# A gated two-block kernel: the first weight group of the first feed-forward is rounded four plan steps and fetched five plan steps further on in the prologue

## The chip, the core and the metric

The kernel runs on one core of a Trainium2 chip. The metric is the device time of one execution in microseconds (us); several executions are timed and the median is taken. Engines are named as the profile names them: PE (matrix products), PEld (its weight loads), DVE (vector), ACT (scalar functions), POOL, and SP, whose queue issues nearly all transfers. A name with a q behind it (SPq, DVEq) is that engine's instruction queue.

## What is computed

Four batches of 512 tokens with 512 features pass through two blocks. Each block adds a gated attention-like term and then a gated feed-forward term to the residual x:

```python
x = x + tanh(g_xattn[0]) * xattn0(layernorm(x), ctx, W_k, b_k, ln_gamma, ln_beta)
x = x + tanh(g_ffn[0])   * ffn0(layernorm(x), up, up_bias, down, down_bias)   # weights rounded to 4 bits
x = x + tanh(g_xattn[1]) * xattn1(layernorm(x), ctx, Wq, Wkv, Wout)           # 16 causal heads
x = x + tanh(g_ffn[1])   * ffn1(layernorm(x), W1, W2, W3)                     # silu gate, Hadamard
```

The part that matters here is `ffn0`. Its up matrix (512 x 2048) and its down matrix (2048 x 512) are rounded first: in each block of 32 along the contraction axis the largest absolute value gives a power-of-two scale, and every weight is rounded to a signed 4-bit grid times that scale.

## The kernel before

The weights of `ffn0` are taken in four groups of 512 hidden units. For each group, `quantise(n)` (L485) is a generator whose steps are interleaved with other work. Its first step fetches the raw rows from memory by 16 transfers of 128 KB (L508) into two tiles, half 0 and half 1. Two steps then find the block maxima on DVE (L525 to L534), one for each half. Eight more steps round four quarters k = 0 to 3, two steps for each quarter: the first does L549 to L552, the second L556 to L559. After the quarters 1 and 3 the rounded half is stored to a scratch matrix `qw_d` in memory by eight transfers (L566). `fetch_q(n)` (L571) then loads the two rounded matrices back in the layout that PE wants, as `up_q` and `dn_q`, 1 MB each (L576). The feed-forward's first product in each chunk, `pu`, reads `up_q` and its second, `acc`, reads `dn_q`. The store, the load back and the raw rows of the next group are all on SP's queue, in one order, and the two raw tiles exist once: the rows of group 1 can be fetched into a half only when the stores of that half of group 0 have landed.

The stretch before the first feed-forward product is the prologue. It runs four generators `cross0(b)` (L663), one for each batch, which do the whole first cross-attention of a batch; `keys_values` (L838), which computes the keys and values of the second attention for later and stores them by SP (`k_d`, `v_d`) out of the tiles `kk_ghi`, `kk_glo` (two of each), `spare` and `vv` (two); and `q0 = quantise(0)`. Two steps of the crosses 0, 1 and 2 and one of keys and of q0 (its fetch) are taken ahead. The rest is written out as a plan (L941 to L951): for each k from 0 to 22, one step of cross 0, of cross 1 from k = 3, of cross 2 from k = 6, of cross 3 from k = 10, then of q0, then one or two steps of keys. `in_time(plan, 20)` (L918) traces the plan's entries in that order and ties each entry, on each of PE, DVE, ACT and POOL, behind the last instruction that was traced on that engine up to the entry 20 places before. SP is not tied. Within these ties a scheduler with a simulated timeline orders each engine; earlier traced work goes first among what is ready.

Cross b has, in the order of its steps: context transposes; tokens 0; key projection; tokens 1; key transposes; tokens 2; the Gram matrix with tokens 3 and the variance (L750); `po` (L753); `pg_o` with the product on DVE (L760); the row scales, a chain of small DVE operations that ends at L778; their transpose; four score tiles `v` with their maximum on DVE (L792) and exponential on ACT (L796); the residual update (L809); squares (L818); scaling; and the layernorm's rows and four transposes. Cross 0's last step is at k = 22.

After the plan, `ffn0((0,), 0, (1, 5))` (L956) starts on batch 0 and group 0. Its first product `pu` goes into a PSUM bank that cross 2 used before (the two banks "h"). Beside its chunks run the steps of `quantise(1)`, one for each chunk, and the rest of the crosses and keys. The tiles of `up_q` take turns with `spare` and the transposed key weights, and the tiles `ghi`, `glo` of the feed-forward are those of `kk_ghi`, `kk_glo`.

Of the kernel before, what the change touches and what calls it, by code (L numbers as in the profile page):

```python
# [42 lines left out]
def flamingo_kernel(  # L43
# [410 lines left out]
    with ExitStack() as l0:  # L454
# [180 lines left out]
        with ExitStack() as xa:  # L635
# [300 lines left out]
            def fetched(n):  # L936
                fetch_q(n)
                yield
# [3 lines left out]
            for k in range(23):  # L942
                plan.extend([crosses[b] for b in range(NB) if k >= 3 * b + b // 3])
                if k == 6:
                    plan.extend([crosses[3]] * 2)
                if k > 4:
                    plan.append(q0)
                if k == 14:
                    plan.append(fetched(0))

                plan.extend([keys] * (2 if 1 < k < 11 else 1))  # L951
# [205 lines left out]
    with ExitStack() as l1:  # L1157
# [191 lines left out]
        with ExitStack() as at:  # L1349
# [238 lines left out]
            with tc.manual_schedule(engines={nc.tensor.engine}):  # L1588
                for s in range(-4, 4 * last + 2):
                    n, g = divmod(s, 4)  # L1590

                    u, k = divmod(s + 8, 4)
# [324 lines left out]
```

## Time and profile before

| | before |
|---|---|
| median of 3 runs | 1300.35 us (1293.84 to 1302.87) |
| profiled execution: its time | 1300.33 us |
| its span, from first to last instruction | 1298.6 us |
| PE busy | 1209.8 us, 93% of the span |
| DVE busy | 846.9 us, 65% |
| ACT busy | 551.6 us, 42% |
| DMA, mean | 144 GB/s |
| q0's first maximum on DVE (L525) | from 24.41 us |
| q0's last rounding operation (L559) | 72.08 to 73.30 us |
| load back of up_q / dn_q issued | 81.91 / 84.42 us |
| first feed-forward product (`pu`) | 118.13 us |

The profile is one execution on the chip. Times are counted from the span's start. Busy time of PE is modelled, so a busy PE is not a PE at its peak. In a row of the timeline the columns are start, duration, engine, line, operation, output<-inputs, shapes and count; a bracket at its end gives the idle time of the engine just before it and what ended it. The chain is the work that ended last, followed back from the end, with start, duration and what it was.

### The profile page before, as it was taken

The numbers are of one execution on the slowest core, as the hardware profiler recorded it, in microseconds if no ns is written. First come the engines' busy times: TensorE is split into PE (matmuls) and PEld (weight loads), VectorE is DVE, ScalarE is ACT, GpSimd is POOL, SyncE is SP. The second block draws the span as 40 slices with busy tenths as digits, with TensorE's granted clock in tenths as the row PEclk, the third lists the DMA queues.
The fourth block names the chain that finished last, engine by engine and source line by source line (L and its number), as shares of the span: only waits on it lengthen the run. The fifth ranks groups of instructions, "written<-read, shape, count | busy, mean of one in ns | idle before, by whom it ended". The sixth has DMA issues, their size and how long they took to land.

```text
span 1298.6 us, 17523 instructions
## 1 busy us (share of the span) xinstructions
PE 1209.8 (93%) x6097; PEld 906.8 (70%) x6097; DVE 846.9 (65%) x1772; ACT 551.6 (42%) x1040; POOL 350.6 (27%) x480
## 2 busy tenths in 40 slices
PE   5998899999999899898989799999999999999998
PEld 4545677878677675565646477777777788888886
DVE  5876897896947665455455656777677754555556
ACT  4559742333433455454445742444334632122210
POOL 1000010000000235445344133444444533333330
PEclk9999999999999899898998799999999999999999
DMA  8792575354153655355340144554434544433421
GB/s 202 282 237 100 73 150 134 98 146 130 25 165 121 190 160 160 101 155 146 93 127 10 49 162 179 195 195 162 172 145 159 222 160 172 171 146 146 154 82 65
DMA packets 113203, 186.43 MB, mean 144 GB/s; under 512 B 13229, under 2 KB 65581, under 8 KB 107995
## 3 DMA queue, kind: packets, MB, share of 16 engines
q1 hardware_dynamic: 110754, 185.04, 45.4%
q8 instruction: 48, 0.79, 0.3%
q10 hardware_dynamic: 2360, 0.28, 0.2%
q14 instruction: 41, 0.33, 0.1%
HBM read 109.22 MB, written 75.80 MB: 142 GB/s over the span
## 4 chain that ended last, share of the span: by engine, by line
PE 64%; DVE 13%; DMA 10%; ACT 6%; issue 2%; SPq 2%; POOL 1%; DVEq 0%; ACTq 0%; POOLq 0%
PE acc L135 12%; PE pS L135 11%; PE pA L135 9%; PE pu L135 5%; PE pp L140 4%; PE acc L595 3%; PE sT L1404 3%; PE sc L409 3%; PE pav L1436 3%; PE den L1444 2%; PE pq L140 2%; DMA w_d<-fw 2%; DMA q_d<-qq 1%; DMA k_d<-kk_glo 1%; DVE fw L284 1%
## 5 line engine op out<-in xcount | busy, mean ns | idle before, releaser
L135 PE MATMUL pS<-tok,pack 128*128 128x512 f32 x768 | 194.8, 399 | 0.0
L135 PE MATMUL acc<-w2T,gg 128*128 128x512 f32 x768 | 183.9, 392 | 5.7 <-DVE x L1790 5.5
L135 PEld LDWEIGHTS acc<-w2T,gg 128*128 128x128 f32 x768 | 142.9, 188 | 39.1 <-DVE x L1790 9.5
L135 PEld LDWEIGHTS pS<-tok,pack 128*128 128x128 f32 x768 | 142.8, 189 | 32.9
L135 PE MATMUL pA<-tok,pack 128*128 128x512 f32 x576 | 152.8, 404 | 0.0
L1790 DVE SCALAR_TENSOR_TENSOR x<-acc,tg,x 128x512 f32<-128x512 f32 x128 | 95.7, 749 | 63.8 <-PE acc L135 63.4
L135 PE MATMUL pu<-xnT,up_q 128*128 128x512 f32 x512 | 131.0, 401 | 6.1 <-DMA up_q<-qw_d 2.3
L420 DVE CUSTOM_DVE_ANT_0 junk<-sc,mask 128x512 f32<-128x512 f32 (+1 forms) x128 | 79.5, 621 | 81.0 <-PE sc L409 76.7
L1408 ACT ACTIVATE e<-sT 128x384 f32<-128x384 f32 (+1 forms) x192 | 95.4, 524 | 76.3 <-PE sT L1404 73.3
L135 PEld LDWEIGHTS pA<-tok,pack 128*128 128x128 f32 x576 | 109.1, 192 | 24.5
L135 PEld LDWEIGHTS pu<-xnT,up_q 128*128 128x128 f32 x512 | 96.0, 190 | 30.1 <-issue 3.0
L1414 POOL TENSOR_SCALAR_AFFINE_SELECT e<-e 128x128 f32<-128x128 f32 (+1 forms) x192 | 62.6, 331 | 143.6 <-ACT e L1408 140.8
L1832 ACT CAST gg<-s 128x512 fp32r<-128x512 f32 x64 | 39.7, 622 | 109.5 <-POOL s L1829 96.9
L409 PE MATMUL sc<-stk 96*128 96x128 f32 (+3 forms) x256 | 80.7, 357 | 5.8 <-ACT e L1408 1.9
L1829 POOL TENSOR_TENSOR s<-s,p 128x512 f32<-128x512 f32 x15 | 19.7, 1316 | 241.4 <-DVE p L1827 137.4
L1404 PE MATMUL sT<-stk 98*128 98x512 f32 (+3 forms) x256 | 80.7, 360 | 3.1 <-ACT e L1408 2.6
L1833 POOL TENSOR_TENSOR gg<-s,gg 128x512 fp32r<-128x512 f32 x60 | 77.2, 1304 | 6.8 <-ACT gg L1832 6.8
L595 PE MATMUL acc<-dn_q,glo 128*128 128x512 f32 x192 | 75.8, 395 | 1.0 <-DVE glo L618 1.0
L614 ACT ACTIVATE ghi<-pu,up_b 128x512 fp32r<-128x512 f32 x48 | 33.1, 689 | 101.0 <-PE acc L595 82.4
L595 PE MATMUL acc<-dn_q,ghi 128*128 128x512 f32 x192 | 75.4, 393 | 0.0
L1404 PEld LDWEIGHTS sT<-stk 98*128 98x128 f32 x256 | 46.1, 196 | 31.7 <-issue 12.8
L1822 ACT ACTIVATE s<-s 128x512 f32<-128x512 f32 x64 | 40.4, 632 | 51.9 <-DVE s L1821 51.7
(290 smaller groups left out, 2208.9 us busy)
## 6 DMA issues: line engine op xcount, KB each, us to landing
pack_d<-pack SPq DMA_DIRECT2D x16, 1024.0 KB
pack<-pack_d SPq DMA_DIRECT2D x16, 1024.0 KB
pack_d<-pack SPq DMA_DIRECT2D x16, 768.0 KB
pack<-pack_d SPq DMA_DIRECT2D x16, 768.0 KB
qw_d<-qw SPq DMA_DIRECT2D x64, 128.0 KB
q_d<-qq SPq DMA_DIRECT2D x16, 512.0 KB
st<-in_L_ffn_W_dram SPq DMA_DIRECT2D x32, 256.0 KB
w2T_d<-w2T SPq DMA_DIRECT2D x16, 512.0 KB
```

The costliest lines, as they stand in the source:

```text
L135: nc.tensor.matmul(out, a, b, start=(i == 0), stop=(i == len(terms) - 1))
L140: nc.tensor.matmul(out, a, b, start=(i == 0), stop=(i == len(terms) - 1))
L409: nc.tensor.matmul(sc[:, g, :], qst[:96, g0 + g, ts(i, P)], kst[:96, g0 + g, :w], start=(g == 0), stop=(per == 1),)
L420: nc.vector.tensor_tensor_reduce(junk[:, :w], sc[:, 0, :], mask[:, S - w :], 1.0, -3.0e38, ALU.add, ALU.max, fin[:, i, g0 : g0 + 1],)
L595: nc.tensor.matmul(acc[t], g[:, ts(t, P)], dn[:, f % 4, :], start=(f == chunks[0] and i == 0), stop=(f == chunks[-1] and i == 1 and groups ...
L1404: nc.tensor.matmul(sc[:, at_ : at_ + S - j * P], kst[:98, g, ts(j, P)], qst[:98, g, j * P :], start=True, stop=True,)
L1408: nc.scalar.activation(e[:, ds(EOFF[js[0]], w)], sc, AF.Exp)
L1414: nc.gpsimd.affine_select(diag, diag, [[0, len(js)], [1, P]], ALU.is_ge, 0.0, base=0, channel_multiplier=-1,)
L1790: nc.vector.scalar_tensor_tensor(x[b][:, t, :], acc, tg[:, 3:4], x[b][:, t, :], ALU.mult, ALU.add)
L1822: nc.scalar.activation(s, s, AF.Silu)
L1832: nc.scalar.copy(g[:, 0], s)
L1833: eng.tensor_sub(g[:, 1], s, f32(g[:, 0]))
```

## The change

Two conditions of the plan are changed, and nothing else.

```diff
                 plan.extend([crosses[b] for b in range(NB) if k >= 3 * b + b // 3])
                 if k == 6:
                     plan.extend([crosses[3]] * 2)
-                if k > 4:
+                if k > 8:
                     plan.append(q0)
-                if k == 14:
+                if k == 19:
                     plan.append(fetched(0))
 
                 plan.extend([keys] * (2 if 1 < k < 11 else 1))
```

The ten steps of q0 stand at k = 9 to 18 and no longer at k = 5 to 14, with all that they issue: the two maxima, the eight rounding steps, and 16 stores to `qw_d`, eight after k = 14 and eight after k = 18 (before: after 10 and 14). The two loads of `fetch_q(0)` stand at k = 19 and no longer at 14. Once q0 is at its end, its entries in the plan are empty but still count among the 20 of `in_time`; the plan is four entries shorter (122 for 126). The fetch of q0's raw rows stays ahead of the plan.

## The prediction

> **What bounds the kernel now.** I read the slices of the page first, then the chain over 68 to 119 us, then the timelines of ACT, DVE, SP and PE there. Slices of 32.5 us, busy time in tenths, the first four of which are the prologue:
>
> ```profile
> PE   5998899999999899898989799999999999999998
> DVE  5876897896947665455455656777677754555556
> ACT  4559742333433455454445742444334632122210
> DMA  8792575354153655355340144554434544433421
> ```
>
> From 32 us on PE is at 8 or 9 tenths nearly everywhere, so a time won or lost before the first feed-forward product is carried to the end almost whole, and nothing else is touched: no operation is added or removed. The question is what the move does to the start of `pu` at 118.13 us. DVE is fullest in the second slice, where q0 runs now; the DMA is at 9 in the third (q0's stores, the load back, the rows of group 1) and at 2 in the fourth. The chain through the third slice:
>
> ```profile
> 72.40 6.11 DMA k_d<-kk_glo
> ...
> 80.96 3.41 DMA qw_d<-qw
> ...
> 84.84 11.00 DMA qw<-in_L_ffn_up_kernel_dram
> 95.85 2.67 DMA qw<-n_L_ffn_down_kernel_dram
> 98.53 0.60 ACT kk_ghi L121
> ```
>
> Every DMA piece here is q0's own traffic or a key store behind it. Where the engines feel it (ACT twice, then the first `pu`):
>
> ```profile
> 77.95 0.59 ACT L121 CAST kk_ghi<-pk 128x512 fp32r<-128x512 f32 x1 [1.94 <-DMA k_d<-kk_ghi]
> ...
> 98.05 0.59 ACT L874 COPY vv<-pv 128x512 f32<-128x512 f32 x1 [3.08 <-DMA v_d<-vv]
> ```
>
> ```profile
> 118.13 2.13 PE L135 MATMUL pu<-xnT,up_q 128*128 128x512 f32 x8 [1.83 <-ACT xT L796]
> ```
>
> So `pu` waits for cross 2's exponentials to give back its bank, not for the weights: these were asked for at 81.91.
>
> **The change, part by part.** *The front, 22 to 57 us: 0 (from -2 to 0).* By the tie of 20 entries, q0's first maximum now comes behind cross 0's variance L750. In the row of before that is at 21.84 and the maximum at 24.41, after a wait of 2.21 for its rows, so it can stay. The second maximum moves behind the key split `spare` of batch 1 (43.78 for 30.04). This frees some 2.4 us of DVE around 30 to 40, which buys nothing: ACT stands idle from 32.85 to 38.64 until a `k_d` store has landed, and from 40 to 57 PE has no gap. If that cover were gone, 2 us could be won: the idle 2.39 of PE before 26.36, most of it q0's maximum ahead of a `spare` split.
>
> *The middle: the wait at 77.95.* The key store is queued on SP behind the rows of group 1 (issued 68.06 to 71.8). These need the stores of half 0, which now follow the sixth q0 step at k = 14, so they come later; but the eight stores of half 0 take their place at about 72 to 77 beside the same key stores. DVE stood idle 3.42 us there. I take half, -1.7 (from -3.4 to 0), as the transfers that come are 1 MB like those that leave.
>
> *The wait at 98.05.* The `v_d` store was issued at 89.94, behind up_q, dn_q and five transfers of rows; some 3 MB. In their new places only the rows of half 0 (1 MB, 8 issues of about 0.45 us, now on the move until about 77, as the DMA's rate is 135 to 139 GB/s from 70 to 76 and 308 after) come before 95 us, about 80 to 92. I take the wait as gone: -3.1 (from -5.4, all of PE's gaps between 94 and 100, to 0).
>
> *DVE at 80 to 105.* Three rounding steps come here that were done by 73: one first half (0.69 + 0.69 + 0.43 + 0.43 = 2.24) and two second halves (0.43 + 0.69 + 0.69 + 1.22 = 3.03), 8.3 us. By the five slices of 5 us DVE is idle 2.32 + 1.22 + 0 + 2.95 + 0.13 = 6.6 us there. The 1.7 over go onto the small chains of the crosses, which feed ACT, and ACT is full from 98 on: +2 (0, if the idle time serves, to +4.6, if the 2.95 before 100 goes with the stall).
>
> *When the weights arrive.* The tenth q0 step now comes behind cross 2's L778, the end of its row scales:
>
> ```profile
> 72.08 1.22 DVE L559 TENSOR_TENSOR qw<-qc,qcols 128x1024 f32<-128x1024 bf16 x1
> ...
> 102.23 0.16 DVE L778 TENSOR_TENSOR rows<-var,hi 128x4 f32<-128x4 f32 x1
> ```
>
> The first is q0's last operation now. From 102.23 go the 1.7 above and the 2.76 that DVE idles inside that chain before 99.15; the ninth step adds 2.24 into it, the tenth itself 3.03: q0 ends at 103.0 for 73.3. From there to the landing of up_q the trace has the same sequence for group 1: L559 ends at 185.67, then
>
> ```profile
> 185.70 4.35 SPq L566 DMA_DIRECT2D qw_d<-qw  x8
> 190.21 0.40 SPq L576 DMA_DIRECT2D up_q<-qw_d  x1
> 192.51 0.38 SPq L576 DMA_DIRECT2D dn_q<-qw_d  x1
> ```
>
> ```profile
> 197.42 3.07 PE L135 MATMUL pu<-xnT,up_q 128*128 128x512 f32 x9 [2.32 <-DMA up_q<-qw_d]
> ```
>
> 11.7 us. So up_q lands at 114.7; `acc` needs dn_q 6.5 us after the first `pu` (124.63 for 118.13), and dn_q is issued 2.3 us after up_q. If `pu` is to start at 116.3, that leaves 1.6 us: 0 here, but of 30 us of slack almost nothing is left. If L778 gains nothing and both steps and the small chain share DVE (102.23 + 2.24 + 3.03 + 4.5), q0 ends at 112 and up_q lands at 123.7: +5.6. The bounds are 0 and +5.6; the ties are hard and the stall is seen, so I stay at the lower.
>
> *Behind it on SP.* In front of up_q wait the eight stores; behind it now come key stores of batch 3 (issued 102.92 to 104.8), value stores, and the rows of group 1, half 1. Two `ghi`/`glo` tiles of the first chunks (ACT 120.64) are the last `kk` tiles: +1 (0 to +5.8, the longest such wait, at 38.64). The rows of half 1 took 13.7 us from issue at 84.84 to 98.53; issued at 118 they land at 131.7, and L525 wants them at 133.13: 0 (to +3). POOL issues no transfers; ACT's queue issues none after 5.6 us.
>
> **Sum:** -1.7 - 3.1 + 2 + 0 + 1 = -1.8 on 1300.33, the profiled execution's own time, which is the median of the runs (1300.35): 1298.5 us.
>
> [...] The rows: PE is busy 1.55 of the 5 us from 95, and the granted clock of the next 5 us is 0.68. [...]
>
> **The rivals.** *The weights come late (slower).* The place is the first `pu`, the price one us for each us that q0 ends after 118.13 - 11.7 = 106.4. For it: the tie behind cross 2's L778, DVE without spare time at 90 to 95 and 100 to 105, and SP in one order. Against it: DVE idles 1.4 to 2.7 us in each slice after 105, so the tenth step isn't held up for long. With q0 at its end at 115 up_q lands at 126.7, +8.6: 1309. Over 1% (13 us) it takes an end after 119.4.
>
> *The DVE and DMA relief comes whole (faster).* Both waits go (-3.4 and -3.1), the front gives its -2 and the crowding is hidden in what remains: -8.5, 1291.8. For it: the DMA has 2 tenths in the fourth slice to take the traffic. Against it: 16 stores and 18 loads still pass between the same key and value stores, only later.
>
> *Little moves.* The plan is an order of tracing; within the ties the scheduler may put q0 back into DVE's idle time, with its first five steps near their old times. Then the third slice stays as it is: 1300.3. Against it: the ties of the steps 8 to 10 are at 79 to 102 us.
>
> **How the numbers follow.** Forecast 0.55; late weights 0.27; whole relief 0.10; little moves 0.08. A measurement of this kernel can tell about 1%, 13 us, from no change. The forecast and the third rival are within it. Of the late weights I put 0.11 beyond +13 us; of the relief 0.04 beyond -13, where the clock of the rule and PE's other gaps before 40 us would have to come too. Faster 0.04, same 0.85, slower 0.11. The range reaches from the whole relief to the late end at 115, each with the 2.5 us by which the highest run of before lies over the median: 1289 to 1312; outside lie some 0.05 below and 0.12 above.
>
> **What would show it.** Right: q0's last L559 ends at 100 to 106, up_q is issued at 107 to 111, no wait of ACT for `v_d` near 98, `pu` at 114 to 119 and still released by ACT. Wrong: `pu` released by the DMA of up_q and more than 3 us after 118; a `ghi` or DVE's L525 of group 1 waiting for a DMA at 118 to 135; or q0 ending before 85. The forecast fails as a whole if the span moves by more than `pu` does, for then the scheduler has set a later stage otherwise.

## The result, and the profile after

The change made the kernel slightly slower. The changed kernel took 1306.63 us in the median of 20 runs (1299.48 to 1310.74), the kernel before 1300.23 us (1293.84 to 1306.90, 20 runs): ratio 1.0039, 95% interval 1.0023 to 1.0055. Run again in another series it gave 1.0043 (1.0023 to 1.0064). The forecast was 1298.5 us, no difference. The profiled execution of the changed kernel is one of its quick ones: 1302.32 us, span 1300.6.

The slices of its page show where the first 230 us differ; PEclk is the clock granted to PE. Each column is 32.5 us:

```profile
PE   5998889999999899898989789999999999999998
...
DVE  5688879996847665555455546777676754555556
...
PEclk8998989999999899898998789999999999999999
DMA  9766195354143655455340135554444644444421
```

The DMA's peak has gone from the third slice to the fourth, DVE's work has moved likewise: the move took place. The clock row of before has no 8 in its first 13 slices; this one has three in its first six.

The prologue first. The DVE timeline shows q0's last rounding operation, SP's the traffic behind it, PE's the first product:

```profile
104.83 1.22 DVE L559 TENSOR_TENSOR qw<-qc,qcols 128x1024 f32<-128x1024 bf16 x1
```

```profile
106.07 4.37 SPq L566 DMA_DIRECT2D qw_d<-qw  x8
110.61 0.38 SPq L576 DMA_DIRECT2D up_q<-qw_d  x1
```

```profile
118.96 2.10 PE L135 MATMUL pu<-xnT,up_q 128*128 128x512 f32 x8 [1.88 <-DMA up_q<-qw_d]
```

q0 ends at 106.05 us and no longer at 73.30, the load back goes out at 110.61 and no longer at 81.91, and yet `pu` starts only 0.83 us later (118.13 before). Of the slack nothing is left: the releaser is now `up_q`. The 0.83 us are no more than executions differ by: in the six profiles of this case with the prologue of before `pu` starts at 115.4 to 119.4 us, in six with the changed one at 116.8 to 119.6.

Behind `pu` PE is then even ahead: batch 1's residual update ends at 166.33 us, for 169.17 before. The loss comes after that. The timeline of PE for batch 3's layernorm transposes and first products, before:

```profile
174.11 1.03 PE L259 MATMUL pt_f<-ident,xn_f 128*128 128x128 f32 x8
176.82 1.35 PE L259 MATMUL pt_f<-ident,xn_f 128*128 128x128 f32 x8
182.10 5.74 PE L135 MATMUL pu<-xnT,up_q 128*128 128x512 f32 x24
```

and after:

```profile
180.15 1.09 PE L259 MATMUL pt_f<-ident,xn_f 128*128 128x128 f32 x8
184.17 1.94 PE L259 MATMUL pt_f<-ident,xn_f 128*128 128x128 f32 x8 [2.93 <-DVE xnT L122]
187.51 8.42 PE L135 MATMUL pu<-xnT,up_q 128*128 128x512 f32 x24 [1.40 <-DVE xnT L122]
```

Before, the transposes stood among batch 2's `acc` products and nobody waited for them. After, they stand behind the last of these, with nothing else for PE to do: 2.93 and 1.40 us of idle time, and the 24 products behind them take 8.42 us for 5.74. The windows of the two kernels there (columns: PE, PEld, DVE, ACT, POOL busy in 5 us, granted clock, DMA share, GB/s) say why, before:

```profile
180.00:185.00 5.00, 5.00 (x22) 3.60 (x21) 4.97 (x8) 0.74 (x2) 3.69 (x10) 1.00 0.24 43
185.00:190.00 5.00, 5.00 (x24) 4.15 (x23) 4.72 (x9) 2.10 (x4) 0.00 (x0) 1.00 0.57 131
```

after:

```profile
180.00:185.00 5.00, 2.07 (x13) 1.72 (x13) 4.62 (x7) 2.48 (x4) 0.00 (x0) 0.80 1.23 144
185.00:190.00 5.00, 3.60 (x12) 2.71 (x11) 1.38 (x2) 1.17 (x2) 3.82 (x14) 0.50 1.15 203
190.00:195.00 5.00, 5.00 (x17) 3.92 (x16) 2.34 (x3) 2.13 (x4) 0.55 (x2) 0.67 0.93 266
```

PE's share of work falls to 2.07 of 5 us and the clock that is granted next is 0.50, then 0.67. Why the layernorm is late is seen on DVE, in the chain of cross 3's residual update. Before:

```profile
148.15 0.18 DVE L801 RECIPROCAL ssum<-ssum 128x4 f32<-128x4 f32 x1 [1.33 <-ACT xT L796]
...
149.02 0.75 DVE L809 SCALAR_TENSOR_TENSOR x<-xT,ssum,x 128x512 f32<-128x512 f32 x1
```

after:

```profile
149.43 0.18 DVE L801 RECIPROCAL ssum<-ssum 128x4 f32<-128x4 f32 x1 [0.61 <-ACT xT L796]
151.43 0.69 DVE L618 TENSOR_TENSOR glo<-g,ghi 128x512 fp32r<-128x512 f32 x1 [1.82 <-ACT g L616]
...
153.37 0.74 DVE L809 SCALAR_TENSOR_TENSOR x<-xT,ssum,x 128x512 f32<-128x512 f32 x1
```

The scheduler, which had another state of its timeline at the end of the prologue, put a `glo` of the feed-forward between the reciprocal and the update. DVE waits there 1.82 us for ACT, whose `ACT_TABLE_LOAD` takes 1.28 us from 149.41 on, between the two uses of one `pu`, and the update is 4.35 us later. By the end of the layernorm's chain of small operations (L223 at 177.19 for 170.49) it is 6.7 us.

A second place stands far behind, where the second attention passes into the second feed-forward. The order of PE, DVE and ACT differs there in some twenty places, and one wait of PE shows it, before:

```profile
748.34 5.04 PE L140 MATMUL pp<-woT,oT 128*128 128x512 f32 x14 [0.79 <-DVE tok L122]
```

after:

```profile
751.35 7.20 PE L140 MATMUL pp<-woT,oT 128*128 128x512 f32 x20 [2.39 <-DVE tok L122]
```

### The profile page after: what moved, and what is told of

It reads as the page before. It is cut to its first block, busy times and chain, and to the rows that moved or that the text cites. A ratio compares the mean times of both kernels' runs of the same rounds, so it can differ in the third digit from the quotient of the medians.

```text
span 1300.6 us, 17524 instructions
## 1 busy us (share of the span) xinstructions
PE 1214.7 (93%) x6097; PEld 909.5 (70%) x6097; DVE 847.3 (65%) x1772; ACT 552.1 (42%) x1040; POOL 349.3 (27%) x480
```

## The experiments

Four theories run through them. P: the prologue itself costs the time. In the first expectations it is called W (the weights come late). L: batch 3's late layernorm. S: the passage at 737 to 770 us, called the passage below. F came up on the way: the gap at the front of the prologue and the one at 181 to 187, each with a half clock behind it (in the changed kernel 0.50 from 26.01 to 32.84 us and from 183.02 to 193.26; some expectations call it cold). O, named in one expectation, says only that the later orders decide and not the prologue. All were timed against the kernel before on the same chip.

**One step in place of four.**

```diff
-                if k > 4:
+                if k > 5:
...
-                if k == 14:
+                if k == 15:
```

> q0's rounding begins one plan step further on than before (k > 5) and its load back is one step further on (k == 15): a quarter of the change. In the program's order on PE this kernel nevertheless has the four transposes of batch 3's layernorm behind the last `acc` product of batch 2, as the changed kernel has, where before they stand between batch 2's products. Theory L (the loss comes from batch 3's layernorm, late on DVE and so behind batch 2 on PE): the whole loss of the change, +5 us on 1300 (ratio 1.004, from 1.002 to 1.006), and the first `pu` of batch 3 starts 4 to 6 us later than before's 182.10. Theory W (the loss comes from the weights: each step by which the rounding and the load back are late costs its share): a quarter, +1 us (ratio 1.001). Theory S (the loss comes from the other order of the products where the second attention passes into the second feed-forward): this kernel has before's order there, so 0.

Measured: 1310.15 us, ratio 1.0058 (1.0035 to 1.0081). A quarter of the change costs no less than the whole, so the loss isn't counted by the steps. Batch 3's first `pu` is late, with the same two waits ahead of it as in the changed kernel (2.93 and 1.40):

```profile
193.79 8.39 PE L135 MATMUL pu<-xnT,up_q 128*128 128x512 f32 x24 [1.40 <-DVE xnT L122]
```

It was 11.7 us later than before, where 4 to 6 were expected; of these some 4 had been lost by batch 1's end (173.14 for 169.17).

**One step, load back two steps on; two steps, load back three.** The first:

```diff
-                if k > 4:
+                if k > 5:
...
-                if k == 14:
+                if k == 16:
```

> As the one-step kernel (k > 5), but with the load back two steps further on (k == 16) in place of one. Its order on PE has batch 3's layernorm transposes between batch 2's products, as before, and at the passage from the second attention to the second feed-forward the order of the changed kernel. Theory L: no loss, ratio 1.000 (0.998 to 1.002), the first `pu` of batch 3 within 2 us of before's 182.10. Theory W: +1 to +2 us, more than the one-step kernel, since the load back is later. Theory S: the whole loss, +5 us (1.004).

Measured: 1305.64 us, 1.0030 (1.0007 to 1.0052). Batch 3's first `pu` starts at 183.43, as theory L said, but there is a loss. Its passage has the changed kernel's order, and a wait of 2.39 us stands before `pp`. That speaks for a second cause, S.

The second:

```diff
-                if k > 4:
+                if k > 6:
...
-                if k == 14:
+                if k == 17:
```

> The rounding begins two steps further on (k > 6), the load back three (k == 17): about half of the change. The order on PE has batch 3's layernorm transposes between batch 2's products, as before, and at the passage to the second feed-forward it is that of before. Theory L: no loss, ratio 1.000 (0.998 to 1.002; a gain of up to 2 us is possible, since the DMA waits in the prologue shrink), the first `pu` of batch 3 within 2 us of 182.10. Theory W: half of the loss, +2.5 us (1.002), more than the one-step kernel. Theory S: 0.

Measured: 1306.98 us, 1.0042 (1.0023 to 1.0061). This was a miss for theory L: neither of the two orders is that of the changed kernel, and it is as slow. The profile shows another loss, in the prologue: its first `pu` starts at 130.07 us, 11.9 later than before. That profile is of the slowest of its twelve runs (1313.96 us), so how much of this the others lost there is open. Each of these settings is a schedule of its own.

**The load back alone.** q0's rounding stays where it was.

```diff
-                if k == 14:
+                if k == 19:
```

> One half of the change alone: the load back is moved to k = 19 and q0's rounding stays at its old place (k > 4). On PE batch 3's layernorm transposes stand between batch 2's products, as before, and on DVE q0's first maximum is as near the front as before. Theory F (new: two gaps of PE make the loss, each with the cold clock behind it: one at 23 to 27 us, where q0's first maximum stands on DVE ahead of a key split and waits for the raw rows, 4.21 us in the changed kernel against 2.39 before, the other at 181 to 187 us, batch 3's layernorm): 0, ratio 1.000 (0.998 to 1.002). Theory W (lateness of the weights): +1 to +3 us, if the first `pu` then waits for up_q. A ratio over 1.003 would speak against both.

Measured: 1310.95 us, 1.0072 (1.0047 to 1.0098), against all theories. The first `pu`:

```profile
129.63 2.91 PE L135 MATMUL pu<-xnT,up_q 128*128 128x512 f32 x8 [2.52 <-DVE xnT L122]
```

It is 11.5 us late, but not for the weights: its `up_q` went out at 82.70, 0.79 us later than before, and the releaser is DVE's last operation of a layernorm. PE is busy for 1.12 of the 5 us from 100 on and runs at a clock of 0.50 in the next five. So moving two transfers in the plan moved the crosses too.

**Equal turns beside the feed-forward, prologue of the change kept.**

```diff
-            jobs.append(both(crosses[1], both(*crosses[2:], keys)))
+            jobs.append(both(*crosses[1:], keys))
```

> The changed kernel with its prologue untouched; only the turns of the work beside the first feed-forward are dealt out otherwise: crosses 1, 2, 3 and keys one step each in turn, where before cross 1 had every second turn and crosses 2, 3 and keys a sixth each. Cross 3's residual update and layernorm are traced earlier, and its transposes stand between batch 2's products on PE again. Theory L: the loss goes: ratio 1.000 against before (0.997 to 1.002), that is 4 to 7 us under the changed kernel, and the first `pu` of batch 3 at 180 to 184 us. Theory W: the prologue is as late as in the changed kernel, so +5 us (1.004) stays. Theory S: this kernel has before's order at the passage, so 0; the place of batch 3's first `pu` tells it from theory L.

Measured: 1302.55 us, 1.0008 (0.9985 to 1.0030). In this kernel q0 ends at 106.08 and up_q is asked for at 110.72, as late as in the changed kernel; the layernorm is early again, and from 290 us on PE, DVE and ACT have the order of before:

```profile
181.77 5.74 PE L135 MATMUL pu<-xnT,up_q 128*128 128x512 f32 x24
```

The loss is gone. Repeated later:

> The changed kernel with equal turns once more, beside these three: the changed prologue, and neither of the two orders behind it. Theories L and S: 1.001 (0.999 to 1.003). Theory P: 1.004.

Measured: 1300.19 us, 0.9998 (0.9977 to 1.0018). Whether the equal turns hide a loss by a gain of their own was asked by giving them to the kernel before:

> Control for the equal turns: the kernel before, with nothing but the turns of the work beside the first feed-forward dealt out equally to crosses 1, 2, 3 and keys. Theory L and theory F: in before batch 3's layernorm is not late, so the equal turns bring nothing: ratio 1.000 (0.998 to 1.002). If instead the equal turns are a gain by themselves, 0.996 to 0.998, then the kernel with the change and equal turns (1.0008) still holds a loss of 3 to 5 us, and the place of batch 3's layernorm was not the cause.

Measured: 1305.08 us, 1.0026 (1.0008 to 1.0045): no gain but a loss. Its profile is 3 us ahead of before at 540 us and 4 us behind after 760. From 200 us on PE's order is that of before; DVE's differs near 430 and ACT's near 610 and 690. One transposition more at the start of the second attention gives ACT its old order:

> The kernel before with equal turns, which in its profile was 3 to 4 us ahead of before from 200 to 580 us and 4 us behind at the end, with one extra 128 x 128 transposition at the start of the second attention, behind which ACT's order in the attention is that of before (three pairs of instructions no longer swapped). Theory O (the later orders, not the prologue, decide these few us): the lead survives, ratio 0.997 to 0.999. If the lead is lost to the clock's phase and not to the order: 1.002 to 1.003 as without the transposition.

Measured: 1302.28 us, 1.0008 (0.9977 to 1.0038). The lead doesn't come back in the time, and its own profile has no lead at 540 us (1.7 us behind), though up to there the two kernels have one order but for the transposition: the lead was that of one execution. The two intervals overlap, so whether those swaps cost anything stays open.

**The front.** In the profile of the changed kernel PE stands idle for 4.21 us before the third key product, in that of before for 2.39. In both q0's first maximum, which waits for the raw rows, is ahead of a key split on DVE. That maximum was tied further back:

```diff
+            def held(job):
+                with behind(traced()):
+                    next(job)
+                yield
...
-                    plan.append(q0)
+                    plan.append(held(q0) if k == 9 else q0)
```

> The changed kernel, with the first entry of q0 in the plan (k = 9, the first block maximum) tied behind the last instruction traced on each engine until then, and no longer only behind the entry 20 places before. On DVE it moves from before the first `spare` split to behind the second. Theory F: the gap of PE before the third key product (4.21 us, 23.28 to 27.49 in the changed kernel) goes or falls under 1.5 us, the granted clock from 25 to 35 us comes back from 0.60 and 0.72 to over 0.9, and the time falls by 2 to 5 us: ratio against before 1.001 (0.999 to 1.003). Theory L: that gap is caught up by the first `pu`, the loss stays at 1.004, with batch 3's first `pu` at 186 to 189 us. Theory W: 1.004.

Measured: 1306.00 us, 1.0035 (1.0010 to 1.0060). The gap is gone from where it was and stands, longer, a few products further on:

```profile
31.68 1.12 PE L716 MATMUL pc<-ident,c_sb 128*128 128x128 f32 x4 [6.14 <-DMA c_sb<-in_ctx_dram]
```

The front waits for transfers in both places (PE here, DVE's first maximum for 4.73 us in the changed kernel), and the place of the maximum is not what makes the gap. What a gap there costs at the end this run can't tell, since there still is one. Nor is a longer gap shown to come with the change: before the third key product it is 2.39 to 4.96 us in six profiles with the prologue of before, 2.78 to 5.52 in six with the changed one. With both remedies (the two diffs together):

> Both remedies in the changed kernel: the first block maximum tied as in the run with the held maximum, and equal turns beside the first feed-forward. Theory F: both gaps are gone and what the change wins in the prologue's middle is left: ratio 0.997 to 0.999 against before, 1297 to 1300 us. Theory L: as equal turns alone, 1.001 (0.999 to 1.003). Theory W: 1.004.

Measured: 1302.88 us, 1.0004 (0.9983 to 1.0024): as with the equal turns alone.

**The passage by itself.** One extra 128 x 128 transposition at the 60th of the steps of the second attention shifts the scheduler's timeline just enough to change its choice at the passage, and nothing before it. The same line gives the kernel before the changed kernel's order, and the changed kernel that of before:

```diff
-                    head = head_at(s)
+                    head = head_at(s); pn = side([P, P], "pn") if s == 60 else None; [nc.tensor.transpose(pn, ident, ident) for _ in range(1 if s == 60 else 0)]
```

> The kernel before, with one extra 128 x 128 transposition into a spare bank late in the second attention (0.15 us of PE). It shifts nothing in the program's order up to there; behind it, where the second attention passes into the second feed-forward (some 737 to 770 us), PE, DVE and ACT take the order of the changed kernel. Theory S (a part of the loss lies at this passage, where the changed kernel has a wait of PE of 2.39 us before `pp` and a cold clock behind it): +1 to +4 us, ratio 1.001 to 1.003. Theories L and F (all of the loss lies before 200 us): 1.000 (0.9985 to 1.0015).

Measured: 1304.69 us, 1.0029 (1.0004 to 1.0054). The kernel before has the wait now:

```profile
755.43 6.43 PE L140 MATMUL pp<-woT,oT 128*128 128x512 f32 x20 [2.40 <-DVE tok L122]
```

> The counterpart: the changed kernel with the same one transposition, behind which the passage to the second feed-forward has the order of before on PE, DVE and ACT; everything up to the transposition is the changed kernel. Theory S: the loss falls by 1 to 4 us, ratio against before 1.001 to 1.003; PE's wait before `pp` near 750 us is under 1 us. Theories L and F: 1.004 stays, as all of it lies before 200 us.

Measured: 1304.36 us, 1.0030 (1.0007 to 1.0053), with 0.69 us of wait before `pp`. In the same series the changed kernel had:

> The changed kernel once more, beside these three on the same chip, for its loss in this series and for a second profile of it. All theories: ratio 1.004 (1.002 to 1.006). Theory F and theory L expect the same two gaps of PE in its profile (4.2 us before 27.5, and 2 to 3 us before 184) and the half clock behind them; theory S the wait before `pp` near 750.

Measured: 1305.27 us, 1.0043 (1.0023 to 1.0064), with the waits expected (5.52 us in place of 4.2 at the front, 2.93 and 1.40 at 184 to 188, 2.39 before `pp`). The signs fit theory S both times, but the 0.9 us that the changed kernel gains when the passage is mended are not clear of noise, and the larger part of its loss is left. Added to the changed kernel with equal turns, the passage gave:

> The changed kernel with equal turns (1.0008 when it was run alone), with one extra 128 x 128 transposition late in the second attention, behind which the passage to the second feed-forward has the order of the changed kernel. Theory S: 1.003 to 1.004, that is 2 to 4 us over the equal turns alone. Theories L and P: as the equal turns alone, 1.001 (L) or 1.004 for both (P).

Measured: 1302.69 us, 1.0021 (0.9999 to 1.0043), 2.5 us more than the equal turns in the same series, with an interval that just reaches no loss.

**The late layernorm by itself.** The kernel before, all of its prologue kept; only cross 3's row sums are multiplied by 1.0 nine times (or six) before the update:

```diff
                 nc.vector.tensor_scalar(ssum, ssum, tg[:, 0:1], None, ALU.mult)
+                [nc.vector.tensor_scalar(ssum, ssum, 1.0, None, ALU.mult) for _ in range(9 if b == 3 else 0)]
```

> The kernel before, prologue and weights as they were; only cross 3's residual update is made late, by nine multiplications of its 128 x 4 row sums by 1.0, one behind the other on DVE. On PE batch 3's layernorm transposes now stand behind batch 2's last product, as in the changed kernel; the passage to the second feed-forward has the order of before. Theory L (batch 3's late layernorm): +3 to +6 us, ratio 1.002 to 1.005, batch 3's first `pu` at 186 to 192 us for 182.10. Theory S (the passage): 0, at most the 0.5 us that the nine operations take. Theory P (the prologue itself): 0.

Measured: 1304.65 us, 1.0038 (1.0012 to 1.0063). Batch 3's transposes are behind batch 2 and the products behind them slow, without anything of the change:

```profile
186.72 8.02 PE L135 MATMUL pu<-xnT,up_q 128*128 128x512 f32 x24 [1.40 <-DVE xnT L122]
```

> The same with six multiplications in place of nine: batch 3's transposes are behind batch 2 on PE, and the passage to the second feed-forward has the order of the changed kernel. The prologue is that of before. Theories L and S together: the whole loss of the change without the change, ratio 1.004 (1.002 to 1.006). Theory L alone: 1.002 to 1.005, as with nine. Theory P: 1.000.

Measured: 1313.31 us, 1.0099 (1.0065 to 1.0134), more than expected: both orders with the prologue of before cost at least as much as the change.

All of it in one table, by what each kernel has of the three suspects. (The runs with one or two steps, the load back alone and the kernel before with equal turns have prologues or stages of their own and are left out.)

| prologue | layernorm late | order at the passage | ratio to before |
|---|---|---|---|
| changed | no | before | 1.0008, 0.9998, 1.0004 (with the maximum held) |
| changed | no | changed | 1.0021 |
| changed | yes | before | 1.0030 |
| changed | yes | changed | 1.0039, 1.0043, 1.0035 (held) |
| before | no | changed | 1.0029 |
| before | yes | before | 1.0038 |
| before | yes | changed | 1.0099 |

In the first row, all of the moved work is where the change put it, and three measurements give no loss, each to some 0.2%. The other rows agree: where the two orders are the same, the changed prologue is nowhere slower than that of before by more than 0.1%. Theory P is refuted for a loss of the size measured.

Theory L shows in the times (0.30 and 0.38% alone) and in its place: from the first `pu` to batch 3's first it is 68.6 to 71.2 us in the six profiles with the late layernorm and 62.2 to 65.1 in six of this table without it, before's (64.0) among them.

The passage was timed at 0.21 and 0.29% alone, some 3 us, but its profiles do not show so much in its place: from 705 to 800 us the six kernels with the changed order lose from -0.8 to +1.2 us against the profile of before, the five others from -0.2 to +0.3. So its wait is shown, and the size of its cost is not.

The sum of the two is more than the 0.4% of the changed kernel, and 1.0099 is more than their sum; with intervals of 0.2 to 0.3% the shares can't be told closer. In the kernels with the late layernorm DVE's order differs from that of before also in some places between 280 and 340 us and near 430, in the one with nine multiplications ACT's between 540 and 690 too, in the one with six ACT's near 290 and 540; no run separates these from the layernorm itself. No kernel here was faster than the one before.

## Why the prediction was wrong

- **What failed: "a time won or lost before the first feed-forward product is carried to the end almost whole, and nothing else is touched".** No operation was added, and the product did start almost where it was (0.83 us later). But behind it the order of the engines was not that of before. The plan is an input of a scheduler with a simulated timeline, and a prologue that ends in another state makes it choose otherwise at places up to 630 us away. The runs showed the loss there: with the later order restored the moved work shows no loss (1.0008, 0.9998, 1.0004), and the late layernorm under the prologue of before costs as much as the change (1.0038). The prediction named this as the sign of its failure (the span moving by more than `pu`), and gave it no chance and no price. In the chances it should have been a rival on the slower side: of eight other settings of plan and turns tried here, none was faster than before, and six were slower with an interval clear of 1.
- **The weights' arrival: right in kind, 3 us short.** q0's end was put at 103.0, within bounds up to 112, and was 106.05. From there to `pu` it took 12.9 us, for 11.7 in the row of group 1 that served as the measure. Price at `pu`: at most 0.83 us, where 0 was said. The signs set for "right" came (q0's end at 106, up_q asked for at 110.6, no wait for `v_d` near 98, `pu` within 114 to 119) but for one: `pu` was released by up_q and no longer by ACT.
- **The middle: -1.7, right in kind.** No key store holds ACT there any more (its idle 3.17 us before 80.73 end with a maximum of DVE), and PE is busy for all of the 10 us from 75 on, for 8.9 before.
- **The wait at 98.05: gone, and the 3.1 us with it.** ACT no longer waits for `v_d`. PE's work from 95 to 100 us rose from 1.55 to 3.49 of 5 us, but from 100 to 105 it fell from 5.00 to 3.71, with the granted clock at 0.77 and 0.55 (0.97 and 0.68 before). DVE is busy for 5.00 of 5 us in both windows: the ninth rounding step ends at 95.15, the tenth begins at 102.89, and a residual update that ran from 91.72 us now runs from 97.51. The crowding took what the wait had given: its term, +2, was too small, or the two were one term. The bound of -5.4 was a wrong sum; PE's gaps between 94 and 100 us of before are 3.45 us.
- **The front: 0, from -2 to 0, is neither shown nor refuted.** The first maximum could stay where it was, as said. In the profile of the changed kernel its wait is 4.73 us for 2.21, PE's gap 4.21 for 2.39, and the clock from 25 to 30 us 0.60 for 1.00; but with either prologue the gap differs as much from one profile to the next. The run with the maximum held shows that transfers set the front (a transfer of `c_sb` ends 6.14 us of idle time of PE there). The second maximum's rows add up to some 4 us, not 2.4, on which nothing rested.
- **Behind it on SP: the rows of group 1 were right, the +1 did not come.** DVE's maxima of group 1 run at 126.49 and 131.04 us, ahead of before's 128.40 and 133.13, without a wait for a transfer. Nor does ACT wait for one at the first `ghi` (121.54 us).
- **Of the rivals,** the late weights were the nearest in sign, and wrong in place. The sum up to `pu` was -1.8 us for a measured +0.8; that error alone would have been within what a measurement of this kernel can tell from nothing.
- **The clock.** The prediction gives the row of the wait at 98.05, PE busy 1.55 of 5 us and then a clock of 0.68. The chances name "the clock of the rule" for what lies beyond -13: no run shows such a rule, or a gain by it. What the runs showed in its place: the half clock behind that wait, from 99.74 to 103.15 us before, lasts from 97.69 to 104.52 in the changed kernel, though the wait is gone. At the first `pu` the clock is full (1.00 from 115 to 120 us); at batch 3's it is not (0.50 and 0.67 at 185 to 195 us).

## What to carry to other kernels

In a kernel whose order comes from a scheduler, a moved step is two changes: the move, and a new draw of every close choice behind it. Price the second one too, and compare the order of the engines after the moved place before explaining a time by the move, and a wait in several profiles before putting it down to a change. To tell the two apart, keep the move and restore the later order (here, by how the turns are dealt or by one idle transposition), and make the later order without the move; a half-step of the change is no smaller an experiment, as it draws anew as well.

## What the runs showed of the hardware

In the clock records of the profiles of before and of the changed kernel the clock is either full or exactly half. Of the 15 half stretches of before nine last 3.413 us, four 6.827, one 10.240, and one, at the end of the span, 2.817; of the 16 of the changed kernel seven, six and two have the same three lengths, and the last, at the end, 3.442. In each of the two profiles all of them begin at one phase of a grid of 3.4133 us, within 2 ns; the phase against the span's start is 0.75 us before and 2.12 after.

In the 3.413 us ahead of these 31 stretches PE was busy, by the profile's (modelled) account, for 2 to 95% of the time: for 43% or less ahead of 16 of them, for 73% or more ahead of nine. Where full clock followed on full clock, the least busy 3.413 us of the grid have 49%, in either profile. Ahead of 183.02 us in the changed kernel, where 1.78 us of the wait of 2.93 lie, it was 48%, and the clock was half from there to 193.26: a half clock stands here behind a gap under 3 us. A sharp bound the two profiles do not show.

The whole is not small. Over 326 of the 328 runs, each compared with others of its kernel, a mean granted clock lower by one thousandth goes with 0.85 us more of time. The kernel before has 0.969 in the mean of 127 runs, the changed kernel 0.963 in 32. No run parts clock and waits there: behind the new waits the granted clock is 0.50 from 185 to 190 us, for 1.00 before, and 0.50 from 750 to 755 us, for 0.83.

Single profiles must be read with care at this scale. Between 560 and 720 us several profiles lose 3 to 6 us against that of before and others next to nothing: the kernel before with the other passage, whose order there is still that of before, lost 3.8, the changed kernel 0.3.
